# First image's phase of a selective-scan and window-attention kernel: all projections ahead of the convolutions, diagonal products and layouts behind them, loads reissued

## The chip, the cores and the metric

The kernel runs on one core of a Trainium2 chip. The metric is the device time of one execution in microseconds (us); the time given for a kernel is the median of several executions. TensorE (PE in the profile), VectorE (DVE), ScalarE (ACT) and GpSimd (POOL) each run their own instructions in the order written; SP only issues transfers. A line such as L443 is a line of the kernel before.

## The reference

The input is `x`, 8 images of 192 channels by 64 by 64, float32. Layer 0 is a selective scan in four directions, layer 1 a window attention with an MLP. What matters here is how layer 0 begins, for each image:

```python
x = conv1x1(x, W_in)                       # 192 -> 384 channels
x = conv_general_dilated(x, W_dw, (1, 1), 'SAME', feature_group_count=384) + b_dw   # depthwise 3x3
x_proxy = conv1x1(x, W_xd)                 # 384 -> 16
ws, Ls, Us, Ds = (conv1x1(x_proxy, w) for w in (W_w, W_l, W_u, W_d))
xs = stack of x, its transpose, and both flipped     # four directions
out = gate_scan(xs, Ls, *normalize_w(*split(ws, 3)), CHUNK=8) * Us + xs * Ds
y = einsum('bdchw,d->bchw', out, w_m)      # then layernorm over channels, GRN, conv1x1 with W_out
...
x2 = window_attention(layernorm(y)); x2 = x2 + mlp(layernorm(x2))
```

## The kernel before

The kernel is one program in three parts.

**The first image's phase** (L327 to L501) makes the convolved input of image 0 and writes it to DRAM in two layouts, `xs` and `xsT`. It loads constants with `load` (L334 to L344), which alternates between the queue of SP and the queue of ACT, loads the image in four strips `xa` and eight half strips `xb` (L366 to L370), and works in 12 units: three channel tiles `ct` of 128 channels by four strips `u` of 16 rows. For each unit:

- `projected` (L432): four matrix products into the PSUM tile `pin` (two buffers), and an ACT copy into `full[ct]` (L443), the 66 by 66 padded image.
- then the 3x3 depthwise convolution. For nine units (all strips of tiles 0 and 1, and strip 0 of tile 2) `convolved` (L462) makes it on DVE in nine instructions, into `acc` (three buffers). For the last three units `convolved_by_products` (L473) makes it on TensorE: nine products with diagonal matrices `dg` into each of two PSUM tiles `pc`, and an ACT eviction of each into `acc` (L483). The convolution needs one row of the next strip.
- `stored` (L445): three ACT copies (L450 once, L454 twice) into the layouts `sn` and `st` (three buffers each), and two stores by SP, to `xsT` (L451) and `xs` (L457).

The loop at L492 to L500 writes the order by hand: the projection of one unit, then the convolution and the layouts of the unit before it. So ACT's copy of projection n+1 stands in ACT's order behind the layouts of convolution n-1. The nine `dg` tiles are made by ACT ahead of the loop (L487).

**The folding of weights** (L503 to L576, here called the prep) opens two pools of its own, `prep` and `prep_ps`, once the pools of the first phase are closed. It loads `w_dw` (L506), builds `w_cv` (L510), scales `w_g2` (L519), folds a mean into `w_out` (L525), and folds norms and biases into the attention's weights. `bias_row` (L527) loads a row (L531), adds matrix products to it on DVE (L539), adds further rows (L542, L543) and has SP write the result into a row of the weight tile (L544). The 24 products of L566 and the DVE work up to L576 end it.

**The planned part** (from L578) holds the rest: the scan of image b, the windows of image b-1 and the front (projection and convolution) of image b+1 side by side. An in-house planner (`Plan`) models the engines and fixes every engine's order; it starts with `x<-xs` (L762), the load of the first step of the first scan, and with `xt` (L636), the load for image 1's front. The planner sees only its own steps: what comes before them does not enter its order.

Of the kernel before, what the change touches and what calls it, by code (L numbers as in the profile page):

```python
# [23 lines left out]
F32 = mybir.dt.float32  # L24
U8 = mybir.dt.uint8
AF = mybir.ActivationFunctionType
ALU = mybir.AluOpType
AX = mybir.AxisListType
PSUM = bass.MemoryType.PSUM
DRAM = bass.MemoryType.DRAM  # L30

P = 128
B, DM, H, W = 8, 192, 64, 64
DIN, ND, NS = 384, 4, 16
CT = DIN // P
CH = 8
HEADS, HD, WS = 6, 32, 8
HALF = DM // 2
# [6 lines left out]
RG = 32  # L45
# [273 lines left out]
def tile_ss2d_then_window_attention(ctx: ExitStack, tc: tile.TileContext, a: dict, out: bass.AP):  # L319
# [6 lines left out]
    nc = tc.nc  # L326
# [1 line left out]

    const = ctx.enter_context(tc.tile_pool(name="const", bufs=1))

    queues = [nc.sync, nc.scalar]
    n_loads = 0

    def load(name, src=None, rows=None):  # L334

        nonlocal n_loads
        src = a[name] if src is None else src
        shape = list(src.shape)
        t = const.tile([rows or shape[0]] + shape[1:], F32, tag=name, name=name)
        if rows:  # L340
            nc.gpsimd.memset(t[HALF:rows], 0.0)
        queues[n_loads % 2].dma_start(t[0 : shape[0]], src)
        n_loads += 1
        return t  # L344

    def blank(name, shape, value=None, engine=nc.gpsimd):
        t = const.tile(shape, F32, tag=name, name=name)
        if value is not None:
            engine.memset(t, value)
        return t  # L350
# [5 lines left out]
    early = ExitStack()  # L356
    epool = early.enter_context(tc.tile_pool(name="early", bufs=1))

    ident = blank("ident", [P, P])
    make_identity(nc, ident)  # L360

    w_in = load("w_in")
    w_dv = load("w_dv")
    xa = epool.tile([P, H, W], F32, name="xa")
    xb = epool.tile([P, NG // 2, 8, W], F32, name="xb")
    for u in range(NG // 2):  # L366
        nc.sync.dma_start(xa[:, 16 * u : 16 * u + 16, :], x[0, 0:P, 16 * u : 16 * u + 16, :])
        for k in range(2):
            row = 16 * u + 8 * k
            nc.scalar.dma_start(xb[64 * k : 64 * k + 64, u], x[0, P:DM, row : row + 8, :])  # L370
        if u == 0:
            vecs = load("vecs")
    full = [epool.tile([P, H + 2, W + 2], F32, name=f"full{ct}") for ct in range(CT)]
    for t in full:
        nc.vector.memset(t[:, 0 : H + 2 : H + 1, :], 0.0)
# [50 lines left out]
        h.make()  # L426
    with early, tc.tile_pool(name="early_ps", bufs=2, space=PSUM) as early_ps:

        taps = [(dy, dx) for dy in range(3) for dx in range(3)]
        dg = epool.tile([P, 9, P], F32, name="dg")  # L430

        def projected(ct, u):  # L432

            cols = slice(ct * P, (ct + 1) * P)
            pin = early_ps.tile([P, 16, W], F32, name="pin")
            outs = [pin[:, 8 * k : 8 * k + 8, :] for k in range(2)]
            for k in range(2):
                row = 16 * u + 8 * k
                nc.tensor.matmul(outs[k], lhsT=w_in[:, 0, cols], rhs=xa[:, row : row + 8, :], start=True, stop=False)
            for k in range(2):  # L440
                half = slice(64 * k, 64 * k + 64)
                nc.tensor.matmul(outs[k], lhsT=w_in[half, 1, cols], rhs=xb[half, u], start=False, stop=True)
            nc.scalar.copy(full[ct][:, 16 * u + 1 : 16 * u + 17, 1 : W + 1], pin)  # L443

        def stored(ct, u, acc):  # L445

            cols = slice(128 * u, 128 * u + 128)
            xs, xsT = scans[0]
            st, sn = (epool.tile([P, CH, 2, 64], F32, name=n, bufs=3) for n in ("st", "sn"))
            nc.scalar.copy(sn.rearrange("p t k w -> p k t w"), acc.rearrange("p (k t) w -> p k t w", k=2))  # L450
            nc.sync.dma_start(xsT()[:, ct, :, cols], sn.rearrange("p t k w -> p t (k w)"))  # L451
            for k in range(2):
                rows = acc[:, 8 * k : 8 * k + 8, :]
                nc.scalar.copy(  # L454
                    st[:, :, k, :].rearrange("p t (r c) -> p r c t", c=CH), rows.rearrange("p r (c t) -> p r c t", t=CH)
                )
            nc.sync.dma_start(xs()[:, ct, :, cols], st.rearrange("p t k w -> p t (k w)"))  # L457

        def near(ct, u, dy, dx):
            return full[ct][:, 16 * u + dy : 16 * u + dy + 16, dx : dx + W]  # L460

        def convolved(ct, u):  # L462

            acc = epool.tile([P, 16, W], F32, name="acc", bufs=3)
            for n, tap in enumerate(taps):
                w = w_dv[:, ct, n : n + 1]
                if n == 0:
                    nc.vector.tensor_scalar(acc, near(ct, u, *tap), w, b_dw[:, ct : ct + 1], ALU.mult, ALU.add)
                else:
                    nc.vector.scalar_tensor_tensor(acc, near(ct, u, *tap), w, acc, ALU.mult, ALU.add)  # L470
            stored(ct, u, acc)

        def convolved_by_products(ct, u):  # L473

            acc = epool.tile([P, 16, W], F32, name="acc", bufs=3)
            for k in range(2):
                pc = early_ps.tile([P, CH, W], F32, name="pc")
                for n, (dy, dx) in enumerate(taps):
                    row = 16 * u + 8 * k + dy
                    nc.tensor.matmul(  # L480
                        pc, lhsT=dg[:, n, :], rhs=full[ct][:, row : row + 8, dx : dx + W], start=n == 0, stop=n == 8
                    )
                nc.scalar.activation(acc[:, 8 * k : 8 * k + 8, :], pc, AF.Identity, bias=b_dw[:, ct : ct + 1])  # L483
            stored(ct, u, acc)

        for n in range(9):
            nc.scalar.activation(dg[:, n, :], ident, AF.Copy, scale=w_dv[:, CT - 1, n : n + 1])  # L487
        units = [(ct, u) for ct in range(CT) for u in range(NG // 2)]
        by_vector = [(ct, u) for ct, u in units if ct < CT - 1 or u == 0]
        by_tensor = [c for c in units if c not in by_vector]  # L490
        done = 0
        for ct, u in units:  # L492
            projected(ct, u)
            while done < len(by_vector) and by_vector[done] < (ct, u):
                convolved(*by_vector[done])
                done += 1
            while by_tensor and by_tensor[0] < (ct, u):
                convolved_by_products(*by_tensor.pop(0))
        for c in by_tensor:
            convolved_by_products(*c)  # L500
        assert done == len(by_vector)  # L501

    with tc.tile_pool(name="prep", bufs=2) as prep, tc.tile_pool(name="prep_ps", bufs=2, space=PSUM) as prep_ps:  # L503

        w_dw = prep.tile([3 * RG, CT * 4 * 3], F32, name="w_dw")
        nc.sync.dma_start(w_dw, a["w_dw"])  # L506
        id3 = prep.tile([3 * RG, RG], F32, name="id3")
        nc.vector.tensor_add(id3, ident[0 : 3 * RG, 0:RG], ident[0 : 3 * RG, RG : 2 * RG])
        nc.vector.tensor_add(id3, id3, ident[0 : 3 * RG, 2 * RG : 3 * RG])
# [17 lines left out]
        def bias_row(name, dst, products, *more):  # L527

            n = dst.shape[-1]
            row = prep.tile([1, n], F32, name="row_" + name)  # L530
            nc.sync.dma_start(row, a[name])  # L531
            for at in range(0, n, 384):
                m = min(384, n - at)
                ps = prep_ps.tile([P, 512], F32, name="ps_pre")
                for k, (lhsT, rhs) in enumerate(products):
                    nc.tensor.matmul(
                        ps[0:1, 0:m], lhsT=lhsT, rhs=rhs[:, at : at + m], start=k == 0, stop=k == len(products) - 1
                    )
                nc.vector.tensor_add(row[:, at : at + m], row[:, at : at + m], ps[0:1, 0:m])  # L539
            for extra in more:  # L540
                got = prep.tile([1, n], F32, name="more_" + name)
                nc.sync.dma_start(got, a[extra])  # L542
                nc.vector.tensor_add(row, row, got)  # L543
            nc.sync.dma_start(dst[HALF : HALF + 1, 1, :], row)  # L544


        bias_row("b_qk", w_qk, [(n1_b[:, ci : ci + 1], w_qk[0:HALF, ci, :]) for ci in range(2)])

        for j in range(2):
            ps = prep_ps.tile([P, 512], F32, name="ps_pre")  # L550
            for ci in range(2):
# [6 lines left out]
                )  # L558
            nc.vector.tensor_add(b_v[:, j : j + 1], b_v[:, j : j + 1], ps[0:HALF, 0:1])
        bias_row("b_pr", w_pr, [(b_v[:, j : j + 1], w_pr[0:HALF, j, :]) for j in range(2)], "n1_br")  # L560

        ps = prep_ps.tile([P, 512], F32, name="ps_pre")
# [1210 lines left out]
```

## Time and profile before

| what | us |
|---|---|
| median of 3 runs (7610.15 to 7637.82) | 7621.01 |
| profiled execution, its own time | 7623.82 |
| its span (first to last instruction) | 7622.0 |
| mean granted TensorE clock in it | 0.86 of full |
| PE, DVE, ACT, POOL busy | 6699.8, 6364.3, 4896.1, 6229.7 |
| first convolution instruction on DVE (L468) starts | 27.42 |
| first prep instruction on DVE (L508) starts | 181.33 |
| first load of the planned part's scan (L762) is issued | 200.47 |

How to read it: the busy times are sums over the whole span. The first 200 us are where the change is, and there the timeline, which lists instructions in order of time with the idle time before them and what ended it, and the table of windows, which gives busy time by engine in each stretch, say more than the sums. A `SPq` or `ACTq` row is the issue of a transfer, not its duration. Releasers are inferred by the profiler.

### The profile page before, as it was taken

How to read it: one execution, taken by the hardware profiler on the slowest of the kernel's cores; microseconds unless marked ns; L12 is line 12 of the kernel's file. 1: busy time of each engine (PE TensorE's matmuls, PEld its weight loads, DVE VectorE, ACT ScalarE, POOL GpSimd, SP SyncE). 2: the span in 40 equal slices, each digit the busy share in tenths (PEclk: the TensorE clock that was granted, in tenths of full speed). 3: DMA queues.
4: the chain of work that ended last, by engine and by line, in shares of the span. 5: the costliest groups of instructions: out<-in, count | busy, mean ns of one | idle time of the engine just before them, and what ended most of it. 6: DMA issues, size and time to landing. Idle time of an engine off the chain costs nothing. (4 is left out here: it accounts for less than half of the span.)

```text
span 7622.0 us, 141764 instructions
## 1 busy us (share of the span) xinstructions
PE 6699.8 (88%) x50180; PEld 3458.4 (45%) x50180; DVE 6364.3 (83%) x15477; ACT 4896.1 (64%) x9649; POOL 6229.7 (82%) x6333
## 2 busy tenths in 40 slices
PE   5888789988998899888999899988888888888987
PEld 2333344444444444444444444444444444444554
DVE  5687788998899988988888988889899989889643
ACT  2455456765776657675777757766576756666665
POOL 0688888998899988988888888889899989899422
PEclk7888789987988889898998889988888878888999
DMA  3666455312551245312551135411211111111100
GB/s 107 164 174 163 121 139 135 101 51 75 154 145 46 55 134 151 89 46 78 157 139 47 50 105 143 124 50 46 60 50 50 49 59 52 49 45 45 32 22 14
DMA packets 988331, 669.39 MB, mean 88 GB/s; under 512 B 651972, under 2 KB 814215, under 8 KB 987623
## 3 DMA queue, kind: packets, MB, share of 16 engines
q1 hardware_dynamic: 985638, 656.86, 32.1%
q8 instruction: 398, 6.52, 0.4%
q10 hardware_dynamic: 1984, 3.48, 0.2%
q14 instruction: 311, 2.54, 0.1%
HBM read 433.98 MB, written 226.18 MB: 87 GB/s over the span
## 5 line engine op out<-in xcount | busy, mean ns | idle before, releaser
L809 PE MATMUL g<-xe,w_g 32*128 32x512 f32 x3648 | 1171.5, 749 | 224.4 <-DVE dx L968 74.6
L809 PE MATMUL g<-xo,w_g 32*128 32x512 f32 x3648 | 1189.1, 729 | 184.5 <-DVE dx L968 90.9
L866 ACT ACTIVATE ab<-g 128x512 f32<-128x512 f32 x1344 | 784.6, 596 | 393.0 <-PE nb L809 168.9
L897 POOL TENSOR_TENSOR ab<-ab 128x512 f32<-128x512 f32 x672 | 865.0, 1287 | 162.7 <-ACT ab L866 151.0
L929 POOL TENSOR_TENSOR pw<-pw,rr 128x512 f32<-128x512 f32 x672 | 867.4, 1291 | 135.6 <-ACT rr L912 115.4
L914 POOL TENSOR_TENSOR pw<-pw,pq 128x512 f32<-128x512 f32 x672 | 881.0, 1311 | 82.5 <-DVE pq L873 53.2
L918 POOL TENSOR_TENSOR pw<-pw,pq 128x512 f32<-128x512 f32 x672 | 878.1, 1307 | 15.5
L982 POOL TENSOR_TENSOR dx<-dx,hu 128x512 f32<-128x512 f32 x576 | 742.9, 1298 | 112.1 <-DVE hu L973 97.1
L910 ACT ACTIVATE rr<-nb,eps 128x512 f32<-128x512 f32 x672 | 462.0, 687 | 571.7 <-DVE nb L907 569.1
L809 PEld LDWEIGHTS g<-xo,w_g 32*128 32x128 f32 x3648 | 410.5, 208 | 719.3 <-DVE dx L968 192.9
L809 PEld LDWEIGHTS g<-xe,w_g 32*128 32x128 f32 x3648 | 408.9, 212 | 704.8 <-DVE dx L968 173.1
L1628 PE MATMUL lp<-hd,w_f 128*64 128x256 f32 (+1 forms) x2304 | 594.9, 497 | 56.1 <-ACT hd L1614 15.0
L990 POOL TENSOR_TENSOR y<-y,dx 128x512 f32<-128x512 f32 x384 | 597.6, 1563 | 2.2
L696 PE MATMUL lp<-strip,w_cv 128*32 128x256 f32 x8064 | 563.5, 418 | 27.6 <-DMA strip<-pad 19.2
L925 DVE SCALAR_TENSOR_TENSOR nb<-nb,rr 128x512 f32<-128x512 f32 x672 | 464.8, 692 | 142.5 <-ACT rr L912 140.3
L934 DVE SCALAR_TENSOR_TENSOR nb<-nb,pw 128x512 f32<-128x512 f32 x672 | 464.7, 692 | 138.4 <-POOL pw L929 136.2
L907 DVE TENSOR_TENSOR nb<-nb,ab 128x512 f32<-128x512 f32 x672 | 465.3, 692 | 113.1 <-POOL ab L897 103.5
L973 DVE TENSOR_TENSOR hu<-g,hid 128x512 f32<-128x512 f32 x768 | 518.7, 681 | 1.0 <-PE g L809 0.7
L809 PE MATMUL nb<-xe,w_g 32*128 32x512 f32 x672 | 479.1, 800 | 12.5 <-DVE hid L942 12.3
L888 ACT ACTIVATE nb<-nb 128x512 f32<-128x512 f32 x672 | 399.5, 594 | 137.7 <-DVE pq L875 78.2
L980 POOL TENSOR_TENSOR y<-hu,dx 128x512 f32<-128x512 f32 x192 | 246.3, 1289 | 291.7 <-DVE hu L973 289.7
L809 PE MATMUL nb<-xo,w_g 32*128 32x512 f32 x672 | 463.1, 774 | 14.6 <-DVE hid L942 14.6
(221 smaller groups left out, 16684.8 us busy)
## 6 DMA issues: line engine op xcount, KB each, us to landing
strip<-pad SPq DMA_DIRECT2D x1008, 132.0 KB
xd<-xsT SPq DMA_DIRECT2D x384, 256.0 KB
x<-xs SPq DMA_DIRECT2D x64, 768.0 KB
xd<-xs SPq DMA_DIRECT2D x192, 256.0 KB
z<-y SPq DMA_DIRECT2D x64, 768.0 KB
zg<-z SPq DMA_DIRECT2D x64, 768.0 KB
pad<-xin SPq DMA_DIRECT2D x168, 264.0 KB
xsT<-sn SPq DMA_DIRECT2D x168, 256.0 KB
```

What stands on the lines that cost most here:

```text
L696: nc.tensor.matmul(pc()[q * RG : (q + 1) * RG, k * 256 : (k + 1) * 256].rearrange("p (h w) -> p h w", h=4), lhsT=w_cv[:, ct, q, dx, :], rh ...
L809: nc.tensor.matmul(dst, lhsT=w[rows, col : col + P], rhs=xp[rows, :], start=True, stop=True)
L866: lambda r=r: nc.scalar.activation(ab()[:, r, :], g[r](), AF.Abs),
L897: plan("POOL", gp(512), lambda: nc.gpsimd.tensor_add(ab()[:, 0, :], ab()[:, 0, :], ab()[:, 1, :]), w=[ab])
L907: plan("DVE", vec(512), lambda: nc.vector.tensor_add(nb(), nb(), ab()[:, 0, :]), r=[ab], w=[nb])
L914: plan("POOL", gp(512), lambda: nc.gpsimd.tensor_add(one(), one(), pq()[:, 0, :]), r=[(pq, 0)], w=[pw])
L918: lambda: nc.gpsimd.tensor_add(one(), one(), pq()[:, 1, :]),
L929: plan("POOL", gp(512), lambda: nc.gpsimd.tensor_mul(one(), one(), rr()), r=[rr], w=[pw])
L973: lambda: nc.vector.tensor_mul(like(hu(), d), like(pu(), d), state(d, ct)),
L982: plan("POOL", gp(512), lambda: nc.gpsimd.tensor_add(dx(), dx(), hu()), r=[hu], w=[dx])
L990: nc.gpsimd.tensor_add(y, y, dx().rearrange("p (c i) -> p i c", c=CH))
L1628: nc.tensor.matmul(dst[:, at : at + rhs.shape[-1]], lhsT=lhsT, rhs=rhs, **flags)
```

## The change

Five edits, all ahead of the planned part:

1. `load` takes a queue, SP by default. Only `w_in`, `w_dv` and `vecs` are loaded by ACT now, beside the `xb` strips; all other constants go on SP's queue.
2. The pool `prep` is opened together with the first phase, and the four small loads of the prep (`w_dw`, `b_qk`, `b_pr`, `n1_br`) are issued there by SP, ahead of the stores.
3. All 12 projections and their copies come first. The nine `dg` tiles are made by ACT after the fourth copy.
4. Then the nine DVE convolutions with their layouts follow in order. After the fifth, seventh and eighth of them comes one of the three units by products, with its own buffers `acc_p` (two).
5. The prep follows in the same pools, with the PSUM of the first phase. The two rows of `bias_row` are written by ACT's queue instead of SP's.

```diff
-    queues = [nc.sync, nc.scalar]
-    n_loads = 0
-
-    def load(name, src=None, rows=None):
-
-        nonlocal n_loads
+    def load(name, src=None, rows=None, queue=nc.sync):
+
...
-        queues[n_loads % 2].dma_start(t[0 : shape[0]], src)
-        n_loads += 1
+        queue.dma_start(t[0 : shape[0]], src)
...
-    w_in = load("w_in")
-    w_dv = load("w_dv")
+    w_in = load("w_in", queue=nc.scalar)
+    w_dv = load("w_dv", queue=nc.scalar)
...
-            vecs = load("vecs")
+            vecs = load("vecs", queue=nc.scalar)
...
+        prep = early.enter_context(tc.tile_pool(name="prep", bufs=1))
+        w_dw = prep.tile([3 * RG, CT * 4 * 3], F32, name="w_dw")
+        nc.sync.dma_start(w_dw, a["w_dw"])
+        added = {}
+        for name in ("b_qk", "b_pr", "n1_br"):
+            added[name] = prep.tile([1, a[name].shape[-1]], F32, name="row_" + name)
+            nc.sync.dma_start(added[name], a[name])
...
-            stored(ct, u, acc)
+            return acc
...
-            acc = epool.tile([P, 16, W], F32, name="acc", bufs=3)
+            acc = epool.tile([P, 16, W], F32, name="acc_p", bufs=2)
...
-        for n in range(9):
-            nc.scalar.activation(dg[:, n, :], ident, AF.Copy, scale=w_dv[:, CT - 1, n : n + 1])
...
-        by_tensor = [c for c in units if c not in by_vector]
-        done = 0
-        for ct, u in units:
+        for n, (ct, u) in enumerate(units):
             projected(ct, u)
-            while done < len(by_vector) and by_vector[done] < (ct, u):
-                convolved(*by_vector[done])
-                done += 1
-            while by_tensor and by_tensor[0] < (ct, u):
-                convolved_by_products(*by_tensor.pop(0))
-        for c in by_tensor:
-            convolved_by_products(*c)
...
+            if n == 3:
+                for m in range(9):
+                    nc.scalar.activation(dg[:, m, :], ident, AF.Copy, scale=w_dv[:, CT - 1, m : m + 1])
+        for n, c in enumerate(by_vector):
+            acc = convolved(*c)
+            stored(*c, acc)
+            if n in (4, 6, 7):
+                convolved_by_products(CT - 1, (4, 6, 7).index(n) + 1)
+
+        prep_ps = early_ps
...
-            row = prep.tile([1, n], F32, name="row_" + name)
-            nc.sync.dma_start(row, a[name])
+            row = added[name]
...
-                got = prep.tile([1, n], F32, name="more_" + name)
-                nc.sync.dma_start(got, a[extra])
-                nc.vector.tensor_add(row, row, got)
-            nc.sync.dma_start(dst[HALF : HALF + 1, 1, :], row)
+                nc.vector.tensor_add(row, row, added[extra])
+            nc.scalar.dma_start(dst[HALF : HALF + 1, 1, :], row)
```

More of the change, by code (lines that the diff above doesn't have):

```diff
@@ L484, in convolved_by_products @@
             stored(ct, u, acc)
-        for n in range(9):
-            nc.scalar.activation(dg[:, n, :], ident, AF.Copy, scale=w_dv[:, CT - 1, n : n + 1])
         units = [(ct, u) for ct in range(CT) for u in range(NG // 2)]
         by_vector = [(ct, u) for ct, u in units if ct < CT - 1 or u == 0]
-        by_tensor = [c for c in units if c not in by_vector]
-        done = 0
-        for ct, u in units:
+        for n, (ct, u) in enumerate(units):
             projected(ct, u)
-            while done < len(by_vector) and by_vector[done] < (ct, u):
-                convolved(*by_vector[done])
-                done += 1
-            while by_tensor and by_tensor[0] < (ct, u):
-                convolved_by_products(*by_tensor.pop(0))
-        for c in by_tensor:
-            convolved_by_products(*c)
[L501 to L506, printed above, removed]
+            if n == 3:
[7 more added lines that the diff above has]
+        prep_ps = early_ps
         id3 = prep.tile([3 * RG, RG], F32, name="id3")
```

## The prediction

> **What bounds the kernel now.** The sliced page first: POOL and DVE stand at 8 or 9 tenths almost everywhere, but the first slice (0 to 190 us) is different.
>
> ```profile
> span 7622.0 us, 141764 instructions
> ...
> PE   5888789988998899888999899988888888888987
> ...
> DVE  5687788998899988988888988889899989889643
> ACT  2455456765776657675777757766576756666665
> POOL 0688888998899988988888888889899989899422
> ```
>
> See that POOL does next to nothing in slice 1: the planned part has not begun, and this is time paid once, ahead of it. So I read that stretch in a table of windows, 20 us each (columns: PE, PEld, DVE, ACT, POOL busy, granted clock, DMA share, GB/s).
>
> ```profile
> 40.00:60.00 20.00, 10.93 (x16) 3.36 (x16) 19.36 (x16) 6.47 (x7) 0.00 (x0) 0.62 0.38 105
> ...
> 100.00:120.00 20.00, 9.88 (x16) 2.67 (x15) 19.43 (x17) 5.48 (x6) 0.00 (x0) 0.67 0.26 74
> 120.00:140.00 20.00, 17.85 (x36) 7.83 (x37) 9.26 (x8) 6.43 (x8) 0.00 (x0) 0.83 0.37 105
> 140.00:160.00 20.00, 20.00 (x49) 8.53 (x48) 0.00 (x0) 6.48 (x8) 0.00 (x0) 1.00 0.19 52
> 160.00:180.00 20.00, 15.92 (x41) 6.52 (x39) 0.00 (x0) 7.79 (x9) 0.00 (x0) 0.95 0.35 98
> 180.00:200.00 20.00, 9.80 (x34) 7.79 (x35) 9.52 (x29) 0.00 (x0) 0.00 (x0) 0.50 0.16 48
> ```
>
> Three limits follow one another. To about 130 DVE is full (the convolutions). From 130 to 175 TensorE is full and DVE stands still (the units by products). From 181 to 200 a chain of small prep steps runs on DVE and PE. The change lays the second beside the first. The waits up to 205 us name the hand-overs (columns: us in total, times, longest):
>
> ```profile
> PE pin L439 <- ACT full L443: 57.4, 8, 12.8
> DVE id L508 <- DMA xs<-st: 51.7, 1, 51.7
> ...
> ACT acc L483 <- PE pc L480: 30.6, 5, 7.0
> ...
> DVE acc L468 <- ACT full L443: 25.3, 1, 25.3
> ```
>
> PE waits for ACT's copy because that copy stands behind the layouts. The prep's first DVE step waits 51.7 us for the last store, because its pool follows the first phase's pool. The timeline gives the durations and the ends:
>
> ```profile
> 22.46 1.28 ACT L487 ACT_TABLE_LOAD   x1 [22.46 <-DMA temp<-in_temp_dram]
> ...
> 27.42 0.81 DVE L468 TENSOR_SCALAR acc<-full,w_dv,vecs 128x1024 f32<-128x1024 f32 x1 [25.28 <-ACT full L443]
> ...
> 27.44 3.78 PE L439 MATMUL pin<-xa,w_in 128*128 128x512 f32 x4 [12.84 <-ACT full L443]
> ...
> 32.23 1.98 PE L439 MATMUL pin<-xa,w_in 128*128 128x512 f32 x4
> ```
>
> See that ACT is held by its own transfer issues to 22.46, and that the same four products take 3.78 us after a pause and 1.98 us right behind others.
>
> ```profile
> 189.61 0.54 DVE L539 TENSOR_TENSOR row_b_qk<-row_b_qk,ps_pre 1x384 f32<-1x384 f32 x1
> ...
> 200.09 0.36 DVE L576 TENSOR_TENSOR rpb<-rpb,top_b 128x192 f32<-128x192 f32 x1
> 200.47 0.59 SPq L762 DMA_DIRECT2D x<-xs  x1
> ```
>
> L762 is issued as L576 ends: the waits of SP put its 3.7 us there down to L576. The planned part starts at 200.47; what the change is worth is how much earlier that becomes, since the planner's order does not depend on it.
>
> **The change part by part.**
>
> *Start of DVE.* In the trace ACT issues w_dv, eight xb and nine constants, held back by transfers in flight; its last xb is issued by 8.79. After, it issues w_in, w_dv, vecs and the eight xb (two issues of some 0.4 more), so it should be free at about 9 to 10, and with the table load of 1.28 at about 11. PE ends the first projection at 11.62 (L442 at 10.28 for 1.34), limited by the arrival of xa and xb; w_in changes queue, but the same bytes go first. The copy L443 takes 1.05, so DVE starts at 11.62 + 0.15 + 1.05 = 12.8 instead of 27.42. The page "DMA: Bandwidth & Descriptors" of the Trainium skill (Issuing engines are not separate DMA queues) speaks against this edit: transfers run on the same 16 engines whoever issues them, and the choice saves only issue time, usually small. Taken so, ACT would be free about when it is now: 22.46 + 1.28 + 1.05 = 24.8, and the sum below would lose 12. The bytes do stay the same, but the row at 22.46 shows that here the issuing sequencer is the cost, since ACT's first copy stands behind it; I take 12.8. Bounds: 11 if x comes earlier, 20 if 18 loads on SP crowd it.
>
> SP gets nine constants more and four small loads: 13 issues at 0.31 to 0.45, about 5 us, behind xa. It ends now at 27.76; I expect 30 to 35. SP's first store comes at 47, so this is hidden; without that cover it would cost its 5.
>
> *Projections in a row.* Back to back one takes 3.0 (32.23 to 34.15 for L439, then 1.08 for L442). The second ends at 14.6 in the trace, as x arrives. Ten more: 14.6 + 30 = 44.6; last copy by 45.8. ACT has 12 copies of 1.05 and nine dg tiles of 0.30 in this time, 15.3 of 33, so it keeps up. Most projections in the trace followed a pause and took 5.7 (27.44 to 31.15 and 2.0). With 5.7 each the last copy would end at 11.6 + 11 x 5.7 + 1.2 = 75.5. The page "TensorE: Matmul & The Clock Gate" (The HAM clock gate) says that the clock halves after an idle window of about 3.4 us and doubles after as much sustained work. The rows at 27.44 and 32.23 agree in size, and the window 140 to 160, with no pause, has a clock of 1.00. I take 3.0; 75.5 becomes a rival.
>
> *DVE chain.* A convolution takes 11.36 (L468 starts at 50.14 and at 61.50). Three fill the acc buffers: 12.8 + 34.1 = 46.9. The fourth needs the layouts of the first, which now wait for all copies: 45.8 + 2.9 (38.90 to 41.83) = 48.7, a new stall of 1.8. Six more: 48.8 + 68.2 = 117.0, against 129.5 now (118.14 + 11.36).
>
> *Products beside it.* One unit takes 2 x 7.73 on PE (158.63 to 166.35), and up to 2 more after a pause. The first is made from 45 to 62 and evicted behind the fifth layouts, at 75; the second from 75 to 93, evicted at 98; the third from 98 to 115.5. ACT then evicts it, lays it out (116.3 to 119.3), and does the last DVE unit: 119.3 + 2.9 = 122.2. SP's last store is issued at 122.3; at the 290 GB/s that the four last transfers of 0.5 MB can take together, and from row 177.70 to the landing at 181.1, they land at about 126. The 46 us of products are thus hidden by DVE, with the ACT tail 5 us behind DVE. If all products ran at half clock, they would add 15 per unit and the tail would be some 50 later.
>
> *Prep.* Its DVE steps no longer wait for stores: they start at 117.0, not 181.33. From there to L539 the trace has 8.28, of which 1.36 is the wait for w_dw, now loaded long before: 6.9, so 123.9. From L539 to L762 it has 10.86, with PE's 24 products (6.23) in it; the 0.52 wait for n1_br goes but stands beside those products, so nothing is gained. 123.9 + 10.9 = 134.8. The stores (126) are in time for L762.
>
> *Rows written by ACT.* ACT waits for DVE at about 124.5 and 128, with only a table load and the first xin copies (after PE's L653, later than 136) queued behind: nothing. SP, freed of them, issues xt right after the stores, which are 8 ahead of need: nothing either. From below: if L762 need not wait for the prep's end (its buffers lie over the first phase's pool, not over prep), it goes at 126, but the products on x queue behind L566 and L653 on PE, at about 137.6 instead of 134.8 + 6.5 = 141.3: 4 gained at most.
>
> *Sum.* 200.5 - 134.8 = 65.7 us: 12.4 by the earlier end of the convolutions and 51.8 by the prep no longer behind products and stores (181.33 - 129.5), with 1.4 for the w_dw wait. The profiled execution has a span of 7622.0 and its own time of 7623.82, 2.8 above the median of 7621.0; its span becomes 7556.3, its time 7558, and the median 7555.3.
>
> **The rivals.**
>
> *Half clock in the projections* (chance 0.09). The evictions or x pace PE so that pauses remain. For it: 8 waits of L439 end with L443 (57.4 us in all), and the window 40 to 60 has a clock of 0.62. Against: with two pin buffers and a copy of 1.05 in a 3.0 period no pause is left. Layouts start at 75.5, the fourth convolution at 78.4, 29.6 later: a gain of 36, 7585.
>
> *ACT stays late or x arrives late* (0.08): DVE starts at 20 to 25, a gain of 54 to 58; 7563 to 7567.
>
> *The prep's end doesn't hold L762* (0.15): 4 more, 7551.
>
> *The planned part loses more than the phase gains* (0.04, slower). The planned part has PE at 88% busy and a granted clock of 0.86 that changes slice by slice. Its place in time moves by 66 us; if the grant came out lower all along, it would grow. Worked: 7421 us times 1.2% is 89, which makes 7644. It decides from about 0.01 of clock, if PE bound the whole of it. Against: POOL and DVE are as full as PE, and three runs of the same program, with whatever grants they had, lie within 28 us.
>
> *Nothing changes* (0.05): the layouts behind the copies, or the third unit's eviction ahead of the last layouts, hold the stores until 185; then L762 stays near 190 to 200. The ACT rows (12 layouts of 2.9 and six evictions of 0.69, 39 us, from 46 to 122) leave room, so this is unlikely.
>
> **How the numbers follow.** The case worked out has 0.59 and gives 7555, by itself 7540 to 7570, which is the spread of the runs (-11, +17) around it. With the case of 4 more the low end is 7537. The half clock case has 7585 and is taken in: 7590. Less than 2 in 10 is left outside. About 0.3%, 23 us, is what a measurement of this kernel can tell from no change. Faster by more takes in the first, the half clock, the late start and the 4-more case: 0.91. Within: 0.05. Slower: 0.04, the loss in the planned part.
>
> **What would show it.** In the changed profile: L468's counterpart starts at 11 to 15; 12 projections end by about 46 with about 2.0 for four L439 products; a short DVE wait before the fourth convolution; no DVE wait for xs<-st; PE products at 45 to 62, 75 to 93, 98 to 116; the first x<-xs at about 135; then the same 21 us to the first gates. It would be wrong if x<-xs came after 160, if the fourth convolution waited 20 us or more, or if the planned part, from x<-xs to the end, were not 7421 within some 20.

## The result, and the profile after

The changed kernel takes 7564.8 us (median of 4 runs, 7549.6 to 7569.2), the kernel before 7626.0 in its runs beside it (4, 7610.2 to 7637.8). The medians differ by 61.2; the ratio is 0.9913, with an interval of 0.9894 to 0.9931: between 53 and 81 us faster. Later runs of the same pair gave 0.9905 (0.9886 to 0.9924) and 0.9922 (0.9907 to 0.9937). Over all executions of this case, 12 of the changed kernel have a mean of 7562.3 and 31 of the kernel before one of 7629.3. So the gain is 67.0, with a standard error of about 2 if the executions count as independent.

The sliced page first. The first slice of POOL and of ACT is where the difference lies:

```profile
span 7566.1 us, 141748 instructions
...
PE   7888799898989889888999899989888888888987
...
DVE  6777788988899889898888988889899988889643
ACT  3555367765677567675776757776667656666765
POOL 1888788998899989987988888889899989899422
```

The windows (columns: PE, PEld, DVE, ACT, POOL busy, granted clock, DMA share, GB/s) show the same work in another arrangement:

```profile
20.00:40.00 20.00, 20.00 (x56) 6.79 (x56) 19.37 (x16) 9.62 (x16) 0.00 (x0) 1.00 0.51 122
40.00:60.00 20.00, 20.00 (x50) 8.00 (x48) 19.42 (x16) 10.42 (x11) 0.00 (x0) 1.00 0.57 158
60.00:80.00 20.00, 5.11 (x8) 2.02 (x7) 19.50 (x17) 9.88 (x11) 0.00 (x0) 0.60 0.48 133
...
100.00:120.00 20.00, 17.17 (x42) 6.97 (x40) 19.39 (x22) 9.46 (x12) 0.00 (x0) 0.93 0.48 134
120.00:140.00 20.00, 14.97 (x64) 9.34 (x64) 7.04 (x23) 3.95 (x6) 0.00 (x0) 0.52 0.65 198
```

DVE is full from 20 to 120 (19.4 to 19.5 of every 20 us), and TensorE's products lie inside that time. From 20 to 60 PE is full at a clock of 1.00, where the kernel before had 0.62 in its window 40 to 60. The waits up to 145 us (total, times, longest) name what is left:

```profile
PE pc L483 <- ACT acc_p L486: 18.9, 2, 14.9
...
DVE acc L471 <- ACT full L446: 12.6, 1, 12.6
ACT L446 <- DMA xb<-in_x_dram: 12.4, 1, 12.4
```

The waits of the projections for ACT's copy (57.4 us before) and of DVE's prep for the stores (51.7) are gone. PE now waits for evictions, 18.9 us. This costs the phase nothing: PE is done with the units before DVE needs it in the prep, where PE waits for DVE again (7.4 us, to 124.56). The timeline has the ends:

```profile
12.43 1.28 ACT L446 ACT_TABLE_LOAD   x1 [12.43 <-DMA xb<-in_x_dram]
...
14.78 1.16 DVE L471 TENSOR_SCALAR acc<-full,w_dv,vecs 128x1024 f32<-128x1024 f32 x1 [12.63 <-ACT full L446]
...
41.81 1.98 PE L442 MATMUL pin<-xa,w_in 128*128 128x512 f32 x4
...
116.94 0.18 DVE L504 TENSOR_TENSOR id<-ident 96x32 f32<-96x32 f32 x1
...
126.66 0.59 SPq L755 DMA_DIRECT2D x<-xs  x1
...
154.36 0.69 DVE L835 TENSOR_TENSOR hid<-g,x 128x512 f32<-128x512 f32 x1 [19.56 <-PE g L802]
```

The last row is where DVE first uses a gate product of the scan, to make `hid`; it is called the first gate product here. In the kernel before it stands at 223.14:

```profile
223.14 0.69 DVE L842 TENSOR_TENSOR hid<-g,x 128x512 f32<-128x512 f32 x1 [22.70 <-PE g L809]
```

So the first phase, the prep and the start of the scan together became 68.8 us shorter. This row is the ruler for all experiments. The source behind the prep is the same in both kernels, and so is the order that it fixes for every engine.

One word on counts: a float32 product stands as two records in these traces. The two products of L442 are x4, the 18 of a unit are x36, and what is called the 24 products of the prep, here and above, is 24 records of 12 products.

The two first profiles differ by only 55.9 in span. The part behind the ruler took 7398.9 before and 7411.7 after in these two executions, and the experiments had to tell whether that is scatter or a loss.

### The profile page after: what moved, and what is told of

It reads as the page before. It is cut to its first block, busy times and chain, and to the rows that moved or that the text cites. A ratio compares the mean times of both kernels' runs of the same rounds, so it can differ in the third digit from the quotient of the medians.

```text
span 7566.1 us, 141748 instructions
## 1 busy us (share of the span) xinstructions
PE 6688.9 (88%) x50180; PEld 3440.8 (45%) x50180; DVE 6362.5 (84%) x15477; ACT 4893.1 (65%) x9649; POOL 6227.0 (82%) x6333
## 5 line engine op out<-in xcount | busy, mean ns | idle before, releaser
L907 POOL TENSOR_TENSOR pw<-pw,pq 128x512 f32<-128x512 f32 x672 | 881.6, 1312 | 85.6 <-DVE pq L866 55.9
L1621 PE MATMUL lp<-hd,w_f 128*64 128x256 f32 (+1 forms) x2304 | 599.2, 502 | 55.9 <-ACT hd L1607 15.0
L935 DVE TENSOR_TENSOR hid<-lx,nb 128x512 f32<-128x512 f32 x672 | 454.1, 676 | 4.9
```

The costliest lines, as they stand in the source:

```text
L907: plan("POOL", gp(512), lambda: nc.gpsimd.tensor_add(one(), one(), pq()[:, 0, :]), r=[(pq, 0)], w=[pw])
L1621: nc.tensor.matmul(dst[:, at : at + rhs.shape[-1]], lhsT=lhsT, rhs=rhs, **flags)
```

## The experiments

Each kernel is the changed one with the edit shown.

**Queues as before.** Constants alternate between SP and ACT again.

```diff
-        queue.dma_start(t[0 : shape[0]], src)
+        queues[n_loads % 2].dma_start(t[0 : shape[0]], src)
+        n_loads += 1
```

> Undoes the first edit alone: constants alternate between the queues of SP and ACT again. Read is the start of the first convolution step on DVE (14.78 after the change) and of the first gate product onto hid on DVE (223.14 before, 154.36 after). Theory (ACT's own issues hold its first copy): ACT is free at about 22.5, table load 1.28, copy 1.05, so DVE starts at 24.9, 10 later, and the first gate product comes at 164; all of it passes on, since DVE bounds the phase. Rival (the issuing engine does not matter, all transfers share the same engines): DVE starts at 14 to 16 and the first gate product stays at 154 to 156. Span: planned part 7406 on top, so 7570 against 7560.

Measured: 7580.8 (ratio 0.9934, 0.9919 to 0.9949). The timeline of this kernel:

```profile
21.44 1.28 ACT L451 ACT_TABLE_LOAD   x1 [21.44 <-DMA w_qk<-in_w_qk_dram]
...
23.79 0.81 DVE L476 TENSOR_SCALAR acc<-full,w_dv,vecs 128x1024 f32<-128x1024 f32 x1 [21.64 <-ACT full L451]
```

ACT is held by its issues to 21.44 instead of 12.43. DVE starts 9.0 later, and the first gate product comes at 164.22, 9.9 later. The rival falls: the issuing engine matters here, because ACT's first copy stands behind its issues. DVE's prep starts 10.9 later (127.80), more than the start. The rest is a stall that the changed kernel escapes by 0.4 us: DVE's fourth convolution waits for the layouts of the first, which stand behind all copies.

```profile
60.06 0.81 DVE L476 TENSOR_SCALAR acc<-full,w_dv,vecs 128x1024 f32<-128x1024 f32 x1 [2.11 <-ACT st L462]
```

**Order as before.** Each projection's copy behind the layouts, products last.

```diff
         for n, (ct, u) in enumerate(units):
             projected(ct, u)
...
-        for n, c in enumerate(by_vector):
-            acc = convolved(*c)
-            stored(*c, acc)
-            if n in (4, 6, 7):
-                convolved_by_products(CT - 1, (4, 6, 7).index(n) + 1)
+            if 0 < n <= len(by_vector):
+                acc = convolved(*by_vector[n - 1])
+                stored(*by_vector[n - 1], acc)
+        for u in range(1, NG // 2):
+            convolved_by_products(CT - 1, u)
```

> Undoes the order alone: each projection's copy stands behind the layouts of the convolution before it again, and the three units by products come last; early loads, queues and the joint pool stay. Theory: the DVE convolutions still end at about 117, but the products run from 112 to 161, their last stores land at about 168, PE's 24 products of the prep end at 172; first gate product at 193 (154.36 after the change), 38 later. DVE's prep starts at 117 all the same. Rival (the pools and early loads made the gain, the order did not): 154 to 165. Span about 7599 by the theory.

Measured: first gate product at 193.92; 7603.4 (0.9969, 0.9956 to 0.9981). In its timeline the pauses and the half-speed projections are back, and DVE's prep still starts at 117, while PE is busy to 162:

```profile
30.43 3.78 PE L442 MATMUL pin<-xa,w_in 128*128 128x512 f32 x4 [7.06 <-ACT full L446]
...
115.36 46.62 PE L483 MATMUL pc<-full,dg 128*128 128x512 f32 x108
...
170.39 0.59 SPq L755 DMA_DIRECT2D x<-xs  x1
```

So 39.6 of the 68.8 hang on the order. Slow projections alone cost nothing here: DVE did not wait for them.

**Products last, projections first.**

```diff
-            if n in (4, 6, 7):
-                convolved_by_products(CT - 1, (4, 6, 7).index(n) + 1)
+        for u in range(1, NG // 2):
+            convolved_by_products(CT - 1, u)
```

> Keeps the projections first and moves the three units by products behind all nine DVE convolutions. Theory: PE makes the first unit early (45 to 60), but its eviction stands in ACT's order behind the last DVE unit (120); the second and third run on PE from 121 to 154, stores land at 160, the prep's products on PE end at 164, first gate product at 186, 32 later than after the change. So of what the order is worth (38 by the run with both undone) the placing of the products is nearly all. Rival (projections first are what counts): 160 or less here. Span about 7592 by the theory.

Measured: first gate product at 183.51; 7593.4 (0.9949, 0.9934 to 0.9963). The waits up to 190 us of this kernel:

```profile
PE pc L483 <- ACT acc_p L486: 59.9, 1, 59.9
...
DVE row_b_qk L534 <- PE ps_pre L531: 30.7, 1, 30.7
```

PE waits 59.9 us for one eviction that stands behind the last DVE unit in ACT's order, and DVE then waits 30.7 us for PE in the prep. So 29.2 of the order's 39.6 are the placing of the products, in ACT's order above all. The other 10.4 go with the projections: with them in a row one unit is made early, and the last product ends at 153.30 here against 161.98 with the order as before. The ruler came 2.5 earlier than I had it, most of it in the prep: PE came to it without a pause, its 24 records took 5.27 us instead of 6.23, and they ended at 161.75 where I had 164.

**The prep in pools of its own, behind the phase.** Its four small loads move there with it (not shown in the cut).

```diff
-        prep = early.enter_context(tc.tile_pool(name="prep", bufs=1))
...
-        prep_ps = early_ps
+    with tc.tile_pool(name="prep", bufs=1) as prep, tc.tile_pool(name="prep_ps", bufs=2, space=PSUM) as prep_ps:
```

> Undoes the joint pool alone: the prep gets pools of its own behind the first phase, and its four small loads are issued there, all four at once; rows are still written by ACT. Theory: DVE's prep waits for the last store to land (about 125.5) and for w_dw (2 more), so it starts 9 later than now and ends at 145.5; the first scan load is again held by the prep's end, since its buffers lie over the prep's; first gate product at 168, 13 later. Second theory (only the late start counts, the scan load is not held): 164 to 165. Rival (the prep's wait is hidden behind the loads of the planned part): 154 to 157. Span about 7574 by the theory.

Measured: first gate product at 167.17, 12.8 later; 7578.9 (0.9934, 0.9918 to 0.9950). The timeline:

```profile
125.92 0.19 DVE L503 TENSOR_TENSOR id<-ident 96x32 f32<-96x32 f32 x1 [9.37 <-DMA xs<-st]
...
145.01 0.36 DVE L568 TENSOR_TENSOR rpb<-rpb,top_b 128x192 f32<-128x192 f32 x1
...
145.39 0.59 SPq L754 DMA_DIRECT2D x<-xs  x1
```

The prep starts 9.0 later, and the first scan load is again issued as the last prep step ends. With the joint pool it is issued 8.1 before that step ends (126.66; the step starts at 134.44 and takes 0.36). So the place of the prep's buffers decides two waits, not one: its own start, and that of the scan load behind it.

**Rows written by SP.**

```diff
-            nc.scalar.dma_start(dst[HALF : HALF + 1, 1, :], row)
+            nc.sync.dma_start(dst[HALF : HALF + 1, 1, :], row)
```

> Undoes the last edit alone: the two rows are written by SP's queue again. Theory (worth nothing or 1 us): SP waits for DVE's rows at about 124.6 and 127.5, so the loads of xt go at 128 to 130.6 and the first scan load at 131 instead of 126.7; the products on x still queue on PE behind the 24 products of the prep and the first front products (xt lands at about 133), so the first gate product onto hid comes at 154 to 156 (154.36 after the change). Rival (SP's wait passes on): 158 to 159, the 4.4 by which the scan load is later.

Measured, one run: first gate product at 154.14 with the scan load at 130.80 instead of 126.66. The 4.1 later load is covered by PE, which comes to the products on x at 138.94 here and at 138.88 after the change. In this one run the edit is worth nothing to the phase. Its single time, 7581.0, is above all of the changed kernel's; with nothing in the phase to explain it and one run only, I draw nothing from it.

**Four convolutions made twice.** Nothing is left out; DVE repeats itself.

```diff
-            for n, tap in enumerate(taps):
+            for n, tap in list(enumerate(taps)) * (2 if twice else 1):
...
-            acc = convolved(*c)
+            acc = convolved(*c, twice=n < 4)
```

> Makes each of the first four DVE convolutions twice (the same result written again): four times 11.29, so 45 us more on DVE, and nothing else. It asks whether time in the first phase passes on one to one. Theory: first gate product at 199.5 (154.36 plus 45.2), and the planned part behind it as long as ever, a span less that start of 7400 to 7420, so a median near 7608. Rival (the planned part shrinks when it starts later, as 7399 against 7412 in the first two profiles suggests: 19 us less per 100 later): 7400 behind it on average, a median near 7601. Second rival (products or layouts set the end, DVE has slack): first gate product under 190.

Measured: first gate product at 200.17, 45.8 later; 7609.9 (0.9967, 0.9955 to 0.9978), 49 above the changed kernel on the same chip (7560.8). DVE had no slack, and time in the phase passes on; the rival of a shorter planned part had 7601.

**All four units of tile 2 by products.** This version was run after the next one, the "version with POOL" that its expectation names.

```diff
-        by_vector = [(ct, u) for ct, u in units if ct < CT - 1 or u == 0]
+        by_vector = [(ct, u) for ct, u in units if ct < CT - 1]
...
-            if n in (4, 6, 7):
-                convolved_by_products(CT - 1, (4, 6, 7).index(n) + 1)
+            if n in (2, 4, 5, 6):
+                convolved_by_products(CT - 1, (2, 4, 5, 6).index(n))
```

> The step between the change and the version with POOL: all four units of tile 2 by products, DVE keeps eight, but all of the prep stays on DVE. First gate product, theory (DVE's prep behind its last convolution bounds the end): DVE starts the prep at 105.7, its first row addition comes at 112.7, the 24 products end at 121, first gate product at 143. Rival (the stores bound it, as in the version with POOL): 141, the same as there.

Measured: first gate product at 142.59, and 7545.7 (7535.2 to 7549.2), against 7561.8 (7559.4 to 7566.9) for the changed kernel on the same chip. Its ratio to the kernel before is 0.9902 (0.9885 to 0.9918), against 0.9922 (0.9907 to 0.9937). The profile places it 11.5 earlier, the medians 16. The two intervals overlap, so the gain over the changed kernel rests on the four runs each, which do not overlap, and on the 11.5.

```profile
105.64 0.18 DVE L504 TENSOR_TENSOR id<-ident 96x32 f32<-96x32 f32 x1
...
115.36 6.23 PE L559 MATMUL ps_pre<-n_gb,w_f 128*128 128x1 f32 x24
```

DVE starts the prep 11.3 earlier with one convolution less, and the same 24 records follow, as the theory had it. The end lies between the theory's 143 and the rival's 141 and nearer the theory; PE comes to the front's products at 121.89 straight behind the 24 records, so the stores do not bound it here.

**The same, and scalings on POOL.** The steps for `w_cv`, `w_g2` and the last of `w_out` go from `nc.vector` to `nc.gpsimd`.

> Goes on from the change: all four units of tile 2 are made by products (after the third, fifth, sixth and seventh DVE convolution), DVE keeps eight, and the scalings of w_cv, w_g2 and w_out go to POOL, which is idle then. Theory (DVE's nine convolutions and the prep behind them bound the phase): DVE ends its convolutions at 105.6 (117), PE its products at 106.5, the 24 products of the prep end at 117, stores land at 116.5, first gate product at 139, 15 earlier than after the change; span near 7547. Rival (PE becomes the bound): its products end at 115 or later and the first gate product comes at 148 to 154.

Measured: first gate product at 140.74 (139 by the theory); 7557.9 (7547 by the theory), ratio 0.9902 (0.9885 to 0.9920), beside 7560.8 for the changed kernel. The phase is 13.6 shorter, the medians differ by 3. Both kernels stand again in the next batch:

> The version with four units by products and scalings on POOL again, beside the changed kernel: its first gate product comes 13.6 us earlier (140.74 against 154.33). Theory (the phase passes on whole): its median is 13 to 14 below that of the changed kernel. Rival (the planned part gives it back): within 4.

> The changed kernel again, for the comparison on this chip: 7555 to 7570; 66 to 69 below the kernel before if the phase's gain passes on whole, 58 to 63 if a tenth of it is given back.

Measured: first gate product at 142.69, 7553.9 (0.9912, 0.9897 to 0.9927) beside 7561.8. So moving the scalings to POOL brought 0 to 2 in the phase over the version without it (142.59): PE waits 4.9 us for the loads of `xt`, which stand behind the last store in SP's order, so the stores bound the end by then. And POOL's help was not free. While POOL made `w_cv`, one DVE step took 2.96 us instead of 1.28:

```profile
33.68 2.18 POOL L506 TENSOR_TENSOR w_cv<-id,w_dw 96x1152 f32<-96x1152 f32 x1 [16.33 <-DMA w_dw<-in_w_dw_dram]
...
33.98 2.96 DVE L473 SCALAR_TENSOR_TENSOR acc<-full,w_dv,acc 128x1024 f32<-128x1024 f32 x1
```

The second profile has the same (2.96 again). DVE's eight convolutions so end at 107.41, against 105.64 without POOL, and the last store is issued at 114.68 instead of 113.38.

Neither theory nor rival was met in the medians: the version lies 3 and 8 us below the changed kernel, where the theory had 13 to 14 and the rival at most 4. I found no cause in the traces, and with four runs a side and a spread of 8 us per execution it stays open.

**The changed kernel again.**

> The changed kernel itself, for a comparison on one chip. First gate product at 154.4; theory (gain of the phase passes on whole): 66 to 69 below the kernel before; rival (some of it is given back later): 52 to 58 below.

Measured: 7560.8, 74 below the kernel before in that batch (7634.4), beyond both theory and rival; in the third batch, 7561.8 against 7624.1, 62 below, where the rival had 58 to 63. The kernel before alone moves by 10 between batches, so these two do not decide.

**Does the phase's gain pass on whole?** The ruler can be taken from the median of each kernel; what is left is the planned part, with the 1.8 us by which a time exceeds the span of its execution:

| kernel | first gate product | median minus it | runs |
|---|---|---|---|
| before (four batches) | 223.1 | 7402.9, 7406.2, 7411.3, 7400.9 | 4, 9, 11, 7 |
| four twice | 200.2 | 7409.8 | 8 |
| order as before | 193.9 | 7409.5 | 6 |
| products last | 183.5 | 7409.9 | 4 |
| prep behind | 167.2 | 7411.7 | 4 |
| queues as before | 164.2 | 7416.6 | 4 |
| rows by SP | 154.1 | 7426.9 | 1 |
| changed kernel (three batches) | 154.4 to 154.1 | 7410.4, 7406.4, 7407.7 | 4, 4, 4 |
| four units by products | 142.6 | 7403.1 | 4 |
| the same with POOL | 140.7, 142.7 | 7417.1, 7411.2 | 4, 4 |

A line through all 82 executions has a slope of 0.94 us of time per us of phase, standard error 0.03. With a level of its own for each batch the slope is 0.91 (0.03), and without the kernel before 0.98 (0.05). So the phase passes on nearly whole; a give-back of up to a tenth is neither shown nor excluded. The 12.8 us that the first two profiles lose behind the ruler are within the scatter of single executions: the changed kernel's own 12 lie between 7549.6 and 7569.2. Over all executions the mean less the ruler is 7406.2 before and 7408.0 after, 1.8 apart.

## Why the prediction was right

The forecast was 7555 with 7537 to 7590, and the measured 7564.8 lies inside. Of the 9.5 between them 5.0 are the median before, which is 7626.0 with its fourth run and was 7621.0 in the sum. The forecast gain of 65.7 stands beside 61.2 in the first comparison and 67.0 over all executions, and beside 68.8 at the ruler. Step by step:

- *Start of DVE*, forecast 12.8: 14.78. The term that was mis-sized is ACT's release. I let it be free at 9 to 10 and have its table by 11; its issues held it to 12.40. The last `xb` issue ended at 8.83 with `w_in` and `vecs` on SP's queue (the run with the queues as before) and ends at 12.40 with them on ACT's, so moving these two cost 3.6 us, not two issues of 0.4. The weighing itself was right. The page "DMA: Bandwidth & Descriptors" of the Trainium skill (Issuing engines are not separate DMA queues) calls the issue time usually small relative to the transfer. Here the constants' issues on ACT, with their waits for transfers in flight, hold ACT's first instruction to 21.44 instead of 12.43. With them on ACT the prediction had ACT's first copy end at 24.8, and DVE starts at 23.79 with the edit undone.
- *Projections in a row*, forecast 3.0 each and the last copy by 45.8: L442 follows itself every 2.97 (38.84 to 41.81), the last copy ends at 45.93. The clock stayed at 1.00 from 20 to 60, and half speed came back in the kernel with the pauses (3.78). Here the rule that the prediction took from the page "TensorE: Matmul & The Clock Gate" (The HAM clock gate) agrees with the trace. Its size was low for the units: the second one, after a pause of 14.9 us, took 18.53 against 15.72 for the first, 2.8 more where up to 2 was allowed. By estimate some 5.6 us of it ran at half speed, longer than the page's 3.4.
- *DVE chain*, forecast end 117.0, with a stall of 1.8: the prep starts at 116.94. The exact hit is luck, since two errors cancelled: the start was 2 later, and the stall vanished, because the layouts of the first unit were done at 48.8 while DVE ended its third convolution at 49.2. The stall itself is real: with the queues as before it takes 2.11 us.
- *Products beside it*, forecast 45 to 62, 75 to 93, 98 to 115.5: 44.79 to 60.5, 75.40 to 93.9, and from 97.94, the prep's first product at 115.29.
- *Prep*, forecast first row addition at 123.9: 123.97. The 24 records took their 6.23.
- *First scan load*, forecast 134.8: 126.66. This is the step that failed. I took the wait of SP for L576 as a wait that stays when the prep's buffers move, and gave the other reading a chance of 0.15. The run with the prep in its own pools shows both sides: there the load waits for the end, here it does not. The price was small, as that rival said (4 us): the products on x come from PE at 138.88, against 141.3 by the main case and 137.6 by the rival.
- *SP and rows*: SP ended its early issues at 30.7 (30 to 35 forecast); the rows on ACT cost nothing and gained nothing in the phase (one run).
- *The planned part*: not slower by more than the runs can tell. The rival that would have ended above the kernel before has no support.

By undoing one edit at a time, in the phase: order 39.6 (of it the products' placing 29.2), the joint pool 12.8, queues 9.9, rows -0.2. These sum to 62 of the 68.8; the rest shows only when several are undone together, and no run split it.

## What to carry to other kernels

When one engine bounds a stage and a second does its share behind it, look at the third engine that serves both: here ACT's in-order queue decided whether TensorE's part lay beside DVE's or behind it, and a different order of the same instructions moved 40 us. A buffer that lies over another stage's buffers is a wait, for its own stage and for the next one; open the small pool early and its loads and first steps leave the path. Keep transfer issues off the engine whose first instruction starts the chain, and judge a gain in a prologue by a ruler in the trace (a fixed instruction), since the whole time scatters by more than many such gains.

## What the runs showed that I had not expected

- POOL is far slower than DVE on small scalings: the 12 steps of 64x128 on `w_g2` took 17.72 us on POOL, beside DVE's convolutions, and 3.55 on DVE alone, five times as much, where the large sums of this kernel (128x512) differ by less than two (1287 ns at L897 on POOL against 692 at L907 on DVE, before).

```profile
35.85 17.72 POOL L515 TENSOR_SCALAR w_g<-w_g,w_m 64x128 f32<-64x128 f32 x12
```

- The 24 records of one column each in the prep follow TensorE's granted clock too: 6.23 us at 0.50 in the changed kernel, 5.69 at 0.57 with the order as before, 5.27 at 0.64 with the products last, 4.21 at 0.86 in the version with POOL. Their weight loads fill that time (5.97 of 6.23 us). They do not hold the clock: in the second and third of these PE came to them from a clock of 1.00 with hardly a pause. Nor do they raise it: in the changed kernel the front's products follow them at once, and their four records take 3.75 us at a clock of 0.50. So a busy PE in the profile is not by itself the work that brings full clock.

```profile
111.49 4.21 PE L559 MATMUL ps_pre<-n_gb,w_f 128*128 128x1 f32 x24
```

- DVE's first convolution step took 1.16 us while POOL still wrote its constants, and 0.81 in the kernel where it started at 23.79, after POOL was done. In ten profiles it started between 14.73 and 15.06 and always ended at 15.92 to 15.94. With the prep in its own pools it started at 14.61 and took 0.85, and there POOL's constant at 14.86 took 1.06 instead of 0.52. With the step of 2.96 us above, this shows that the two engines hold each other up, now the one, now the other; which pairs of instructions do so, no run was made to tell.
